# GpSimd adds the two states of six groups out of eight, not of four, ahead of TensorE's transposes into y

## The chip, the cores and the metric

The kernel runs on one core of a Trainium2 chip. The metric is the device time of one execution in microseconds. Before the change three runs gave 1902.42, 1903.18 and 1904.25 us, with a median of 1903.18 us. Engine names below are those of the profile: PE is TensorE's matmuls and PEld its weight loads, DVE is VectorE, ACT is ScalarE, POOL is GpSimd, SP is the engine whose queue issues the DMAs.

## The reference

A layer norm of x (4096 tokens, 256 channels, float32) goes into two branches, and their sum is added to x. One branch is a Mamba block (inner width 512, 16 states, a convolution of 4 taps), the other a local transformer of two layers (8 heads of 64, windows of 128 tokens, a gated MLP of hidden width 682). Cut to what the change touches, the Mamba branch:

```python
x_conv = silu(conv(x_inner) + conv_b)
x_dbl  = x_conv @ x_proj_w.T
dt     = softplus(x_dbl[..., :16] @ dt_proj_w.T + dt_proj_b)
B_ssm, C_ssm = x_dbl[..., 16:32], x_dbl[..., 32:48]
dA  = exp(dt[..., None] * A)                       # (l, 512, 16)
dBx = (dt * x_conv)[..., None] * B_ssm[:, None, :]
# for t in order:  h = dA[t] * h + dBx[t];  y[t] = sum over the 16 states of h * C_ssm[t]
y   = y + x_conv * D_param
out = y * silu(z) @ out_proj_w.T
...
return x + mamba(xn) + local_transformer(xn)
```

## The kernel before

The Mamba branch works on blocks of 512 tokens (`TB`, 8 of them) and on chunks of 128 inner channels (4 of them, on the partitions). For one block and chunk the 16 states are taken in 8 groups of two (`GS` = 8, `NG` = 2), so there are 8 x 4 x 8 = 256 groups in all. The transformer works on steps of 256 tokens, 16 for each of its two layers, 32 in all. Both branches run at once, interleaved on every engine.

One group is the function `recur` (line 775):

- L453 (called at 784): two DMAs on the SP queue copy two rows of B and two rows of C to all partitions, into two of the six buffers `bc` ("spreads"). A group holds two buffers, so three groups can be in flight. B's buffer is then written over and over: here it is called u.
- L793: POOL multiplies u (128 x 1024) by `dtx`, which is dt times x_conv.
- for each of the two states: L802 ACT makes the decay exp(dt A) into a PSUM tile `da` (there are two), L807 DVE scans along the tokens, L813 ACT keeps the last column for the next block, L817 DVE multiplies by C into the state's half of u.
- L825, only for groups whose number is in `PAIRED` (line 49): POOL adds the two halves of u into the first one.
- L829, `collect`: PE transposes 128 x 128 tiles of u and accumulates them in the PSUM tile y. There are four transposes for each half that is left: four for a paired group, eight for another. The lines are 823 to 840:

So over all groups and states y is summed by TensorE's accumulation of transposes; where a group is paired, one of its two additions is made by POOL. When the eight groups of a chunk are through, `close` (842) copies y (L846), turns it back (L850), adds x_conv D (L854) and gates it (L859), and `out_proj` (L879) follows after the four chunks. The other POOL work is in the steps of the softplus (L765, L767, L768), in the rotary products and sums of the transformer (L899, L945, L985), and in the MLP's norm and gate (L1149, L1157, L1218).

The order of instructions on each engine is fixed when the program is built, by the class `Plan`. Each piece of work is recorded with an engine, an assumed duration, what it reads and writes, and a key. The key is a place in the pipeline minus a lead, `soon=`, which stands at nearly every call. `Plan.order` (183) runs through the engines and picks, of the work that is ready by its own account of durations and buffers, the one with the smallest key, looking ahead by `AHEAD` at most. The result is five queues (PE, DVE, ACT, POOL, SP), each in order. On the chip an instruction at the head of a queue whose input or buffer isn't ready holds up all that is behind it.

```python
n_sums = 1 if g in PAIRED else NG
if n_sums == 1:
    add("POOL", 1.22, lambda: nc.gpsimd.tensor_tensor(u.ap[:, 0, :], u.ap[:, 0, :], u.ap[:, 1, :], ALU.add), [], [u], soon=-0.37)
...
for i in range(n_sums):
    add("PE", 0.44, lambda i=i: collect(i), [(u, i)], [y], soon=-0.06)
```

Of the kernel before, what the change touches and what calls it, by code (L numbers as in the profile page):

```python
# [42 lines left out]
AHEAD = 2.190000  # L43
# [5 lines left out]
PAIRED = (1, 3, 5, 7)  # L49
# [269 lines left out]
def mamba_and_local_transformer(  # L319
# [135 lines left out]
    def load_small():  # L455
        dma(96, lambda: xpw.ap, lambda: xp_wT.rearrange("(c p) n -> p c n", p=P), writes=[xpw], soon=-0.27)
        for at_row in (0, DH):
            dma(32, lambda at_row=at_row: dtw.ap[at_row : at_row + DTR], lambda: dt_wT, writes=[(dtw, at_row)], soon=-1.3)
        dma(128, lambda: b2row.ap, lambda: b2_d[DEPTH - 1 : DEPTH, :].partition_broadcast(P), writes=[b2row], soon=-0.91)

    def load_qkv(l):
        for s in range(3):
            cut = slice(s * INNER, (s + 1) * INNER)
            dma(
                512, lambda cut=cut: wqkv.ap[:, :, cut],
                lambda cut=cut: wqkv_d[l][:, cut].rearrange("(k p) n -> p k n", p=P), writes=[(wqkv, s)], soon=-0.18,
            )

    def load_rest(l):
        dma(512, lambda: wo.ap, lambda: wo_d[l].rearrange("(h p) n -> p h n", p=P), writes=[wo], soon=-0.99)  # L470
        for half in range(2):
            for m, n in ((0, WHOLE), (NM - 1, LAST)):
                to, of = w1_at(half, m), half * HID + m * MC
                dma(
                    n, lambda to=to, n=n: w1.ap[:, :, to : to + n],
                    lambda of=of, n=n: w1_d[l][:, of : of + n].rearrange("(k p) n -> p k n", p=P),
                    writes=[(w1, (half, m))], soon=0.35,
                )
# [3 lines left out]
            lambda: w2_d[l][0:whole, :].rearrange("(m p) n -> p m n", p=MC), writes=[(w2, 0)], soon=-0.25,  # L482
        )
        dma(42, lambda: w2.ap[0 : HID - whole, NM - 1, :], lambda: w2_d[l][whole:HID, :], writes=[(w2, 1)], soon=0.66)
# [28 lines left out]
        add("PE", 8.3, shift, [w1], [pb], soon=-0.7)  # L513
        add("DVE", 0.4, bias, [pb], [b1, b1x], soon=0.6)
        add("DVE", 4.6, scale, [], [w1], port=True, soon=0.34)
# [14 lines left out]
    def base_of(s):  # L530

        base = plan.value(rows_b)
        if s in sums:
            dma(256, lambda: base.ap, lambda: sums[s].ap, [sums[s]], [base], soon=-0.57)
            return base
        dma(256, lambda: base.ap, lambda: rows(x, s), writes=[base], soon=-1.31)
# [3 lines left out]
            ), [b2row], [base], soon=-0.48,  # L540
# [3 lines left out]
    def finish(s, po, base):  # L544

        add("DVE", 0.6, lambda: nc.vector.tensor_tensor(base.ap, halves(po), base.ap, ALU.add), [po], [base], soon=-1.48)  # L546
        if s in sums:
            dma(256, lambda: rows(out, s), lambda: base.ap, [base], soon=-0.51)
            return
        sums[s] = plan.fixed(dram.tile([P, NW, D], F32, tag=f"sum{s}", name=f"sum{s}"))  # L550
        dma(256, lambda: sums[s].ap, lambda: base.ap, [base], [sums[s]], soon=0.0)
# [4 lines left out]
    def shift_column(l, s):  # L556
        now = xts[l, s]
        if s == 0:
            add("POOL", 0.14, lambda: nc.gpsimd.memset(now.ap[:, 1, 0:1], 0.0), [], [(now, 0)], soon=0.0)
        else:  # L560
# [3 lines left out]
                [(old, 1)], [(now, 0)], soon=-0.52,  # L564
            )

    def normalize(s):
# [5 lines left out]
        dma(256, lambda: xb.ap, lambda: rows(x, s), writes=[xb], soon=0.37)  # L573
# [27 lines left out]
        add("DVE", 1.1, stats, [xb], [mv], soon=1.29)  # L601
        add("ACT", 0.5, root, [mv], [rstd], soon=0.53)
        add("DVE", 0.6, centre, [mv, rstd], [xb], port=True, soon=-0.03)
        now = xts[0, s] = plan.value(tokens)
        add("PE", 0.44, turn, [xb], [pt], holds=[now], soon=0.01)
        add("ACT", 0.48, lambda: nc.scalar.copy(now.ap[:, :, 1:], halves(pt)), [pt], [(now, 1)], soon=0.16)
        shift_column(0, s)
        dma(256, lambda: xn_d[s].ap, lambda: now.ap[:, :, 1:], [(now, 1)], [xn_d[s]], soon=-0.93)
# [3 lines left out]
    def reload(s):  # L612
        now = xts[1, s] = plan.value(tokens)
        dma(256, lambda: now.ap[:, :, 1:], lambda: x1_d[s].ap, [x1_d[s]], [(now, 1)], soon=-1.46)
# [6 lines left out]
    def in_half(i):  # L621
# [3 lines left out]
            lambda: in_wT[:, i * DI : (i + 1) * DI].rearrange("(k p) n -> p k n", p=P), writes=[w], soon=-1.21,  # L625
# [3 lines left out]
    def in_proj(b, w, c, to):  # L629
# [9 lines left out]
        add("PE", 1.72, emit, [w, xms[b]], [pm], holds=[to], soon=-0.6)  # L639
        return pm  # L640

    def front_load(b):
        xm = xms[b] = plan.value(xms_b)
        for i in range(PB):
            s = b * PB + i
            dma(
                256, lambda i=i: xm.ap[:, :, i * TS : (i + 1) * TS], lambda s=s: xn_d[s].ap, [xn_d[s]], [(xm, i)], soon=0.29
            )
# [4 lines left out]
    def front_conv(b, c, w):  # L653
        xin, xc, tail = plan.value(rows_m), xcs[b], tails[b]
        edge = slice(c * (TAPS - 1), (c + 1) * (TAPS - 1))
        if b == 0:
            add("POOL", 0.14, lambda: nc.gpsimd.memset(xin.ap[:, 0 : TAPS - 1], 0.0), [], [(xin, 0)], soon=0.12)
        else:
# [3 lines left out]
                [(old, c)], [(xin, 0)], soon=0.95,  # L662
            )
        pm = in_proj(b, w, c, xin)
        add("ACT", 0.48, lambda: nc.scalar.copy(xin.ap[:, TAPS - 1 :], pm.ap), [pm], [(xin, 1)], soon=0.73)
        if b < NB - 1:
            add(
                "POOL", 0.14, lambda: nc.gpsimd.tensor_copy(tail.ap[:, edge], xin.ap[:, TB:]), [(xin, 1)], [(tail, c)], soon=0.09
# [5 lines left out]
            ), [], [pm], soon=-0.15,  # L674
# [8 lines left out]
        for j in range(TAPS - 1):  # L683
            add("DVE", 0.7, lambda j=j: tap(j), [xin, pm], [(xc, c) if j == TAPS - 2 else pm], soon=0.78)

    def silu(v):
# [4 lines left out]
        add("ACT", 4.52, emit, [], [v], soon=0.43)  # L691

    def front_dbl(b):
# [3 lines left out]
        def emit():  # L697
# [9 lines left out]
        add("PE", 1.75, emit, [xc, xpw], [px], holds=[xd, part], soon=-0.32, part="columns")  # L707
        add("ACT", 0.48, lambda: nc.scalar.copy(part.ap[0:n, 0:TB], px.ap[DH : DH + n]), [px], [part], alone=[px], soon=0.25)
        add(
            "DVE", 0.6, lambda: nc.vector.tensor_tensor(xd.ap[0:n], px.ap[0:n], part.ap[0:n, 0:TB], ALU.add),  # L710
            [px, part], [(xd, 0)], alone=[px], soon=-1.5,
        )

        add("ACT", 0.48, lambda: nc.scalar.copy(xd.ap[DH : DH + DTR], xd.ap[0:DTR]), [(xd, 0)], [(xd, 1)], soon=-0.07)
        xds[b] = xd
        bc = bcs[b] = plan.fixed(dram.tile([2 * NS, TB], F32, tag=f"bc{b}", name=f"bc{b}"))
        dma(64, lambda: bc.ap, lambda: xd.ap[DTR:n, :], [(xd, 0)], [bc], soon=0.15)

    def gate_conv(b, c, w):
# [4 lines left out]
        add("ACT", 0.48, lambda: nc.scalar.copy(sz.ap[:, c, :], pz.ap), [pz], [(sz, c)], soon=-0.62)  # L724

    def times(b, c):
# [12 lines left out]
        add("PE", 1.15, emit, [xd, dtw], banks2, holds=dts2, soon=0.77, part="rows")  # L739
        for i in range(2):  # L740
# [3 lines left out]
                ), [banks2[i]], [dts2[i]], soon=0.17,  # L744
# [3 lines left out]
    def prepare(b, c):  # L748

        if c % 2 == 0:  # L750
# [7 lines left out]
        add("ACT", 0.6, lambda: nc.scalar.activation(e.ap[:, n], dt.ap, AF.Abs), [dt], [e], soon=-0.79)  # L758
        add("ACT", 0.6, lambda: nc.scalar.activation(dt.ap, dt.ap, AF.Relu), [], [dt], soon=-1.5)
# [3 lines left out]
            [e], [r], port=True, soon=0.0,  # L763
        )
        add("POOL", 1.22, lambda: nc.gpsimd.tensor_tensor(r.ap[:, n], e.ap[:, n], r.ap[:, n], ALU.subtract), [e], [r], soon=0.43)  # L765
        add("ACT", 0.6, lambda: nc.scalar.activation(e.ap[:, n], e.ap[:, n], AF.Ln, bias=one_t), [], [e], soon=0.53)
        add("POOL", 1.22, lambda: nc.gpsimd.tensor_tensor(dt.ap, dt.ap, r.ap[:, n], ALU.add), [r], [dt], soon=-1.5)  # L767
        add("POOL", 1.22, lambda: nc.gpsimd.tensor_tensor(dt.ap, dt.ap, e.ap[:, n], ALU.add), [e], [dt], soon=-0.88)  # L768
        add(
            "DVE", 0.61, lambda: nc.vector.tensor_tensor(dtx.ap, dt.ap, xc.ap[:, c, :], ALU.mult),  # L770
            [dt, (xc, c)], [dtx], port=True, soon=0.42,
# [3 lines left out]
    def recur(b, c, g):  # L775
# [6 lines left out]
        for s in range(2):  # L782
# [4 lines left out]
                .rearrange("n t -> (n t)").partition_broadcast(P), [bc], [w], soon=-0.78,  # L787
# [7 lines left out]
            ), [dtx], [u], soon=0.16,  # L795
        )
        for i in range(NG):
# [6 lines left out]
                ), [dt], [h], soon=0.96,  # L804
# [4 lines left out]
                ), [(u, i), (state, (c, n))], [h], soon=-1.03,  # L809
            )  # L810
            if b < NB - 1:
                add(
                    "ACT", 0.1, lambda h=h, n=n: nc.scalar.copy(state.ap[:, c, n : n + 1], h.ap[:, TB - 1 : TB]),  # L813
                    [h], [(state, (c, n))], alone=[h], soon=0.0,
# [4 lines left out]
                ), [h, spread[1]], [(u, i)], alone=[h], soon=-0.19,  # L819
# [4 lines left out]
        if n_sums == 1:  # L824
            add("POOL", 1.22, lambda: nc.gpsimd.tensor_tensor(u.ap[:, 0, :], u.ap[:, 0, :], u.ap[:, 1, :], ALU.add), [], [u], soon=-0.37)  # L825
# [13 lines left out]
        for i in range(n_sums):  # L839
            add("PE", 0.44, lambda i=i: collect(i), [(u, i)], [y], soon=-0.06)  # L840

    def close(b, c):
# [3 lines left out]
        add("ACT", 0.48, lambda: nc.scalar.copy(ytv(), y.ap), [y], [yt], soon=-0.97)  # L846

        def turn():
# [3 lines left out]
        add("PE", 0.44, turn, [yt], [py], soon=0.0)  # L852
# [3 lines left out]
            ), [py], [(xc, c)], soon=-1.5,  # L856
# [3 lines left out]
            [sz], [(xc, c)], soon=-1.24,  # L860
        )

    def out_load():
# [3 lines left out]
            writes=[w], soon=1.12,  # L867
# [3 lines left out]
    def out_proj(b, i, w):  # L871
# [12 lines left out]
        add("PE", 3.44, emit, [w, xc, base], [po], soon=-0.93)  # L884
# [5 lines left out]
    def rotation(l, s):  # L890
# [3 lines left out]
            writes=[rot], soon=0.02,  # L894
        )
        for i, scales in enumerate((qks, qkw)):
            for q in range(2):
# [6 lines left out]
                    ), [rot], [(trig, (i, q))], soon=-0.19,  # L904
# [3 lines left out]
    def project(l, s, t):  # L908
# [3 lines left out]
        def matmuls(q, holds):  # L912
# [10 lines left out]
            add("PE", 1.72, emit, [xb, (wqkv, q)], [pm], holds=holds, soon=0.19)  # L923
# [4 lines left out]
        def norm(q, pm, sq):  # L928
            add("ACT", 0.48, lambda: nc.scalar.activation(sq.ap, pm.ap, AF.Square), [pm], [sq], alone=[pm], soon=0.53)
# [3 lines left out]
                ), [sq], [(nrm, q)], soon=-0.7,  # L933
# [10 lines left out]
        def turned(parts, to):  # L944
            add("POOL", 1.22, lambda: nc.gpsimd.tensor_tensor(parts[0].ap, parts[0].ap, parts[1].ap, ALU.add), [parts[1]], [parts[0]], soon=1.16)  # L945
# [9 lines left out]
            add("PE", 0.44, emit, [parts[0]], [pt], holds=[to], soon=0.36)  # L955
# [458 lines left out]
```

## Time and profile before

| | |
|---|---|
| median of three runs | 1903.18 us |
| the profiled execution's own time | 1899.32 us |
| its span, first to last instruction | 1897.5 us |
| mean granted TensorE clock | 0.993 |
| busy: PE / PEld / DVE | 1855.4 / 1423.5 / 1724.6 us |
| busy: ACT / POOL | 1539.9 / 1410.9 us |
| L829 PE, transposes into y | 1536 instructions |
| L825 POOL, the addition of two states | 128 instructions |
| L793 POOL, u by dtx | 256 instructions, 606.0 us |
| L807 DVE, scans (two forms) | 512 instructions, 639.8 us |
| share of time in which the DMA queue's packets run | 52.5% |

The profile is that of one execution. A matmul's recorded duration overlaps the next one's, so the busy time of PE is larger than what PE must spend; the distance between the starts of matmuls that follow each other without a wait tells the latter. A row of groups has the line, engine, operation and shapes, the count, the busy time and the mean duration in ns of one, then the idle time ahead of these instructions and what ended it. A row of waits has who waited, for what, the total in us, the number of times and the longest.

### The profile page before, as it was taken

To read this page: it belongs to the slowest core of one execution; us is meant where nothing else is said; L and a number is where in the kernel's file an instruction comes from. 1 tells how busy PE (TensorE), PEld (TensorE's weight loads), DVE (VectorE), ACT (ScalarE), POOL (GpSimd) and SP (SyncE) were. 2 spreads that over 40 slices of the span, in tenths; PEclk is the share of its full clock that TensorE was granted. 3 is DMA by queue.
4 is the path that set the end of the run, shared out by engine and by line. 5 is a ranking of instruction groups with operands and counts; after the bars stand their busy time and mean duration, and the time that the engine had idled before them with its cause. 6 is when DMAs were issued, how large, how long until landed. Compare 5 with 4: busy or idle time off the path is not lost. (4 is left out here: it accounts for less than half of the span.)

```text
span 1897.5 us, 35612 instructions
## 1 busy us (share of the span) xinstructions
PE 1855.4 (98%) x12432; PEld 1423.5 (75%) x12432; DVE 1724.6 (91%) x3190; ACT 1539.9 (81%) x3634; POOL 1410.9 (74%) x1178
## 2 busy tenths in 40 slices
PE   7999999999999999999999999999999999999997
PEld 4777777877777778778778787778777787777786
DVE  6799999999998999989998898998999989998996
ACT  5897988888878788788886888888898878888773
POOL 3676888777877778867787676887768877787874
PEclk9999999999999999999999999999999999999998
DMA  5453655554555455555555644556444564544654
GB/s 188 139 194 114 221 166 180 180 173 166 198 167 182 145 170 194 163 187 185 191 184 191 216 152 162 169 189 222 152 160 163 191 214 159 180 160 155 217 173 144
DMA packets 133956, 334.69 MB, mean 176 GB/s; under 512 B 13468, under 2 KB 57200, under 8 KB 133776
## 3 DMA queue, kind: packets, MB, share of 16 engines
q1 hardware_dynamic: 133488, 332.21, 52.5%
q8 instruction: 98, 1.61, 0.3%
q14 instruction: 82, 0.67, 0.1%
q10 hardware_dynamic: 288, 0.20, 0.0%
HBM read 315.06 MB, written 17.30 MB: 175 GB/s over the span
## 5 line engine op out<-in xcount | busy, mean ns | idle before, releaser
L793 POOL TENSOR_TENSOR bc<-dtx,bc 128x1024 f32<-128x1024 f32 x256 | 606.0, 2369 | 144.1 <-DMA bc<-bc 107.1
L807 DVE TENSOR_TENSOR_SCAN da<-da,state,bc 128x512 f32<-128x512 f32 x448 | 563.5, 1278 | 39.7 <-ACT da L802 21.1
L802 ACT ACTIVATE da<-dt,negA 128x512 f32<-128x512 f32 x512 | 348.3, 693 | 78.4 <-DVE bc L817 74.9
L918 PE MATMUL mm<-wqkv,xt 128*128 128x512 f32 x768 | 355.1, 598 | 1.4 <-DVE top L1032 1.2
L817 DVE TENSOR_TENSOR bc<-da,bc 128x512 f32<-128x512 f32 x512 | 339.0, 678 | 5.7 <-ACT state L813 3.4
L1176 PE MATMUL mm<-hn,w 128*128 128x256 f32 (+1 forms) x1408 | 338.2, 383 | 1.3 <-DVE mlp L1226 0.5
L1176 PEld LDWEIGHTS mm<-hn,w 128*128 128x128 f32 (+1 forms) x1408 | 256.8, 189 | 60.2 <-issue 17.0
L1042 ACT ACTIVATE pr<-pr,top 128x256 f32<-128x256 f32 (+1 forms) x512 | 253.2, 500 | 25.9 <-DVE top L1032 25.6
L918 PEld LDWEIGHTS mm<-wqkv,xt 128*128 128x128 f32 x768 | 139.5, 191 | 133.4 <-issue 120.7
L825 POOL TENSOR_TENSOR bc<-bc 128x512 f32<-128x512 f32 x128 | 164.6, 1287 | 88.0 <-DVE bc L817 86.9
L829 PE MATMUL y<-ident,bc 128*128 128x128 f32 x1536 | 214.9, 277 | 8.8 <-POOL bc L825 8.3
L1032 DVE CUSTOM_DVE_ANT_0 pr<-mm,maskf,nrm 128x256 f32<-128x256 f32 (+1 forms) x512 | 213.1, 474 | 9.5 <-PE mm L1017 9.0
L985 POOL TENSOR_TENSOR turn<-turn,trig 128x512 f32<-128x512 f32 x128 | 162.9, 1293 | 65.7 <-DVE turn L978 57.1
L829 PEld LDWEIGHTS y<-ident,bc 128*128 128x128 f32 x1536 | 175.5, 142 | 46.6 <-issue 20.8
L945 POOL TENSOR_TENSOR turn<-turn,turn 128x512 f32<-128x512 f32 x128 | 164.6, 1286 | 51.3 <-DVE turn L963 50.8
L1017 PEld LDWEIGHTS mm<-kT,qT 64*128 64x128 f32 x2016 | 119.9, 187 | 36.1 <-issue 14.4
L1059 ACT COPY prT<-mm 128x512 f32<-128x512 f32 (+1 forms) x256 | 137.0, 591 | 7.0 <-PE mm L1055 6.3
L1055 PE MATMUL mm<-ident,pr 128*128 128x128 f32 x1008 | 135.7, 278 | 3.8 <-ACT qT L956 1.4
L813 ACT COPY state<-da 128x1 f32<-128x1 f32 x448 | 70.1, 165 | 85.1 <-DVE da L807 70.3
L1017 PE MATMUL mm<-kT,qT 64*128 64x128 f32 x2016 | 136.7, 281 | 0.0
L1071 PE MATMUL mm<-prT,v 128*64 128x128 f32 x2016 | 132.2, 278 | 0.7 <-ACT prT L1059 0.2
L1055 PEld LDWEIGHTS mm<-ident,pr 128*128 128x128 f32 x1008 | 117.6, 144 | 18.9 <-issue 4.9
(132 smaller groups left out, 3444.9 us busy)
## 6 DMA issues: line engine op xcount, KB each, us to landing
bc<-bc SPq DMA_DIRECT2D x512, 512.0 KB, 4.4
io<-in_x SPq DMA_DIRECT2D x32, 256.0 KB, 5.0
mw<-in_in_wT SPq DMA_DIRECT2D x16, 512.0 KB, 5.1
rot<-in_rot SPq DMA_DIRECT2D x32, 128.0 KB, 4.2
xn<-xt SPq DMA_DIRECT2D x16, 256.0 KB, 4.0
xm<-xn SPq DMA_DIRECT2D x16, 256.0 KB, 4.2
x<-mid SPq DMA_DIRECT2D x16, 256.0 KB, 3.0
mw<-in_out_wT SPq DMA_DIRECT2D x8, 512.0 KB, 3.7
```

The source lines that it names most:

```text
L793: "POOL", 2.35, lambda: nc.gpsimd.tensor_tensor(u.ap, dtx.ap.unsqueeze(1).to_broadcast([P, NG, TB]), u.ap, ALU.mult), [dtx], [u], soon=0.16,
L802: "ACT", 0.63, lambda h=h, n=n: nc.scalar.activation(h.ap, dt.ap, AF.Exp, scale=negA[:, c * NS + n : c * NS + n + 1]), [dt], [h], soon=0.96,
L807: "DVE", 1.18, lambda h=h, n=n, i=i: nc.vector.tensor_tensor_scan(h.ap, h.ap, u.ap[:, i, :], state.ap[:, c, n : n + 1] if b else 0.0, ALU. ...
L817: "DVE", 0.61, lambda h=h, i=i: nc.vector.tensor_tensor(u.ap[:, i, :], h.ap, spread[1].ap[:, i, :], ALU.mult), [h, spread[1]], [(u, i)], a ...
L825: add("POOL", 1.22, lambda: nc.gpsimd.tensor_tensor(u.ap[:, 0, :], u.ap[:, 0, :], u.ap[:, 1, :], ALU.add), [], [u], soon=-0.37)
L829: nc.tensor.matmul(y.ap[:, t, :], lhsT=u.ap[:, i, t * P : (t + 1) * P], rhs=ident, is_transpose=True, start=g == 0 and i == 0 and t == 0, ...
L918: nc.tensor.matmul(pm.ap, lhsT=hT[k], rhs=wqkv.ap[:, k, q * INNER : (q + 1) * INNER], start=k == 0, stop=k == KC - 1,)
L1017: nc.tensor.matmul(halves(scs[j])[:, i, a * WIN : (a + 1) * WIN], lhsT=qT.ap[half, 2 * g + i, :], rhs=kk.ap[half, 2 * g + i, :], start=n == 0,
L1032: nc.vector.tensor_tensor_reduce(out=prs[j].ap[:, i, keys], in0=halves(scs[j])[:, i, keys], in1=mask[:, keys], scale=nrm.ap[:, h : h + 1], ...
L1042: nc.scalar.activation(prs[j].ap[:, i, keys], prs[j].ap[:, i, keys], AF.Exp, bias=top.ap[:, h : h + 1], scale=-1.0, accum_out=den.ap[:, h ...
L1055: nc.tensor.transpose(ppv()[:, j, a, :], prs[j].ap[:, i, a * WIN : (a + 1) * WIN], ident)
L1176: nc.tensor.matmul(halves(pm)[0:r, i, :], lhsT=w1.ap[:, k, c0 : c0 + r], rhs=hn.ap[:, k, :], start=k == 0, stop=k == KC - 1,)
```

## The change

Line 49 takes groups 0 and 4 into `PAIRED`, so that six groups of eight are paired. In 64 groups more, two for each of the 32 pairs of block and chunk, POOL adds the halves, and PE has four transposes instead of eight. Besides, `AHEAD` and nearly all of the 119 leads have other values, so the order on all five queues is another one. The diff, cut to the lines the text speaks of:

```diff
-AHEAD = 2.190000
+AHEAD = 2.170000
...
-PAIRED = (1, 3, 5, 7)
+PAIRED = (0, 1, 3, 4, 5, 7)
...
-                    writes=[(w1, (half, m))], soon=0.35,
+                    writes=[(w1, (half, m))], soon=-1.38,
...
-                .rearrange("n t -> (n t)").partition_broadcast(P), [bc], [w], soon=-0.78,
+                .rearrange("n t -> (n t)").partition_broadcast(P), [bc], [w], soon=-0.81,
...
                 u.ap, dtx.ap.unsqueeze(1).to_broadcast([P, NG, TB]), u.ap, ALU.mult
-            ), [dtx], [u], soon=0.16,
+            ), [dtx], [u], soon=-0.07,
...
         if n_sums == 1:
-            add("POOL", 1.22, lambda: nc.gpsimd.tensor_tensor(u.ap[:, 0, :], u.ap[:, 0, :], u.ap[:, 1, :], ALU.add), [], [u], soon=-0.37)
+            add("POOL", 1.22, lambda: nc.gpsimd.tensor_tensor(u.ap[:, 0, :], u.ap[:, 0, :], u.ap[:, 1, :], ALU.add), [], [u], soon=-0.86)
...
         for i in range(n_sums):
-            add("PE", 0.44, lambda i=i: collect(i), [(u, i)], [y], soon=-0.06)
+            add("PE", 0.44, lambda i=i: collect(i), [(u, i)], [y], soon=-0.05)
...
-            add("POOL", 1.22, lambda: nc.gpsimd.tensor_tensor(parts[0].ap, parts[0].ap, parts[1].ap, ALU.add), [parts[1]], [parts[0]], soon=1.16)
+            add("POOL", 1.22, lambda: nc.gpsimd.tensor_tensor(parts[0].ap, parts[0].ap, parts[1].ap, ALU.add), [parts[1]], [parts[0]], soon=0.5)
```

In the orders that are built, POOL has on average 7.4 instructions between a group's multiplication (L793) and its addition (L825) before, and 9.0 after; 1.5 of them before and 1.8 after are multiplications of later groups. The first transpose into y stands behind 63.5 us of PE work before and behind 68.2 us after (each instruction counted with its distance between starts, see the prediction). On PE the 96 short matmuls of L495, which read w1, stand ahead of x_dbl's matmuls (L702) after, and behind them before; on the SP queue the four loads of w1 stand behind those of wo and w2 after, and ahead of them before. Behind the last transpose into y both orders have the same 7.8 us of PE work.

## The prediction

> **What bounds the kernel now.** I read the page first: busy times, then the costliest groups.
>
> ```profile
> span 1897.5 us, 35612 instructions
> PE 1855.4 (98%) x12432; PEld 1423.5 (75%) x12432; DVE 1724.6 (91%) x3190; ACT 1539.9 (81%) x3634; POOL 1410.9 (74%) x1178
> L793 POOL TENSOR_TENSOR bc<-dtx,bc 128x1024 f32<-128x1024 f32 x256 | 606.0, 2369 | 144.1 <-DMA bc<-bc 107.1
> L825 POOL TENSOR_TENSOR bc<-bc 128x512 f32<-128x512 f32 x128 | 164.6, 1287 | 88.0 <-DVE bc L817 86.9
> L829 PE MATMUL y<-ident,bc 128*128 128x128 f32 x1536 | 214.9, 277 | 8.8 <-POOL bc L825 8.3
> ```
>
> PE is busy nearly throughout, VectorE 91%; POOL has 487 us free. PE's busy time overstates its need, because a matmul's recorded duration overlaps the next. So I took the timeline of PE in a stretch without a wait and read the distances between starts.
>
> ```profile
> 911.92 0.60 PE L829 MATMUL y<-ident,bc 128*128 128x128 f32 x4
> 912.35 0.60 PE L950 MATMUL mm<-ident,turn 128*128 128x128 f32 x4
> 912.79 0.60 PE L1097 MATMUL mm<-ident,wide 128*128 128x128 f32 x4
> 913.32 2.02 PE L1071 MATMUL mm<-prT,v 128*64 128x128 f32 x32
> 915.27 0.66 PE L829 MATMUL y<-ident,bc 128*128 128x128 f32 x4
> 915.76 1.89 PE L1176 MATMUL mm<-hn,w 128*128 128x256 f32 x8
> 917.49 3.73 PE L1112 MATMUL mm<-OT,wo 128*128 128x128 f32 x32
> 921.06 0.60 PE L829 MATMUL y<-ident,bc 128*128 128x128 f32 x4
> ```
>
> Four transposes take 0.43 to 0.44 us (911.92 to 912.35), 0.109 us each, not the 0.277 of the row; eight matmuls of L1176 take 1.73 us, 0.216 each. Counting every PE group of the page with its distance (768 and 256 of 128x512 at 0.429, 2560 of 128x256 at 0.216, 3568 transposes at 0.109, 1024 of L1112 at 0.111, 2016 + 2016 small ones at 0.060 to 0.064, and some 40 us of the rest) gives 1786 us. PE thus has work for 94% of the span and stands idle 112 us: some 20 before the first transpose into y at 83.6, some 20 after 1850, the rest spread thinly, 7 to 19 us in each stretch of 237. PE is the bound, loosely.
>
> Third, the waits around the addition, SP's own among them:
>
> ```profile
> PEld y L829 <- POOL bc L825: 11.3, 8, 3.8
> PE y L829 <- POOL bc L825: 8.3, 3, 3.5
> POOL bc L825 <- DVE bc L817: 86.9, 42, 6.4
> POOL bc L793 <- DMA bc<-bc: 107.1, 74, 4.9
> DVE da L807 <- POOL bc L793: 12.0, 13, 2.6
> SPq L453 <- PE y L829: 496.7, 195, 8.9
> ```
>
> PE waited 19.6 us (11.3 and 8.3) for 128 additions. The last row says that loads into u are issued when the transposes have let the buffer go: a buffer freed later is a load issued later.
>
> **The change part by part.** *Transposes removed.* 64 groups (2 more of 8, 32 times) lose four each: 256 x 0.109 = 27.9 us off PE, all on the engine that is the bound. The 256 weight loads (142 ns each, 36 us of PEld) lie beside matmuls and count nothing; were they not covered, they would be inside the same 0.109.
>
> PE's row puts a transpose at 277 ns, and the Trainium skill, "TensorE: Matmul & The Clock Gate", Part 4: PE-mode transpose, has about 275 ns for one in a kernel's context; by that the 256 would be worth 70 us. The starts decide against it here: that duration is latency, and neighbours overlap it.
>
> *Additions added.* 64 x 1.287 = 82.4 us on POOL: 1410.9 to 1493, 79%. POOL's own free time hides it; without that cover it would be 82.4 us. What leaks is waiting:
> - PE for the additions. Two of the waits (3.8 and 3.5) are in the last 35 us, around groups that were paired before. Without them 12.3 us stand against some 126 additions, 0.097 each, so 64 more cost 6.2 us. Bounds: 0, and the whole 82.4 if each addition went through.
> - Work queued behind the new additions on POOL: the next groups' L793, the rotary sums L945, L985, and the softplus. For these VectorE waited 12.0 us (L807), PEld 11.6 (L950 for L945), ACT 6.5 (L766 for L765): 30 us. POOL's free time falls from 487 to about 387, a factor 1.26, and if the waits grow by it, 7.8 us come, of which I put half, 4, on PE's path. Bounds 0 to 7.8.
> - The addition waits for L817 at the head of POOL's queue (86.9 us in 128, 0.68 each): 43 us more of POOL standing, still within its free time. Nothing.
> - The buffer u is kept an addition longer; its next load, behind it in SP's queue, comes later. POOL already waits 107 us for such loads, yet only 12.0 us of that reach the scans. Taken as within the 4 us; the slow rival below prices it in full.
>
> VectorE and POOL get in each other's way in a few VectorE instructions:
>
> ```profile
> L770 DVE TENSOR_TENSOR dtx<-dt,xc x32: 673/785/1750, 69.5 to 1833.9; 128x512 f32<-128x512 f32 x32
> L762 DVE TENSOR_SCALAR m2k<-m2k x32: 370/432/2186, 64.6 to 1812.5; 128x512 f32<-128x512 f32 x32
> ```
>
> The three numbers are minimum, median and maximum. The means are 974 and 759 ns, so 32 each lose 9.6 and 12.4 us over the minimum; L589 (363 to a mean of 691, x32) and L972 (140 to 349, x64) lose 10.5 and 13.4. Together 46 us, while the scans and L817 (minimum 634, maximum 693) lose nothing. With POOL 5.8% busier that is 2.7 us more, on an engine with slack: 0 on the path, 2.7 at most.
>
> The Trainium skill, "SBUF — State Buffer", section "SBUF: two separate sides", speaks against giving POOL more: the port pair that it shares with VectorE is locked for a whole instruction and the loser fully blocks. If every VectorE instruction fell under it, 82 us of POOL would be up to 82 us of VectorE. The page limits it to perf modes or two SBUF inputs, and the rows agree: L770 reads two SBUF tiles, L817 has one operand in PSUM.
>
> *Leads and AHEAD.* No work is added, every order moves. At the start 68.2 us of PE work stand ahead of the first transpose into y instead of 63.5; if that fills idle time, 4.7 us are gained. Against it, PE now has L495 (5.2 us in the trace) ahead of L702, and its w1 is loaded after wo and the 640 KB of w2, which took 6.2 us to land; PE, in order, may stand there up to 5 us with L702, x_dbl and the first group behind it. Net 0, bounds -5 to +5. In the steady part the idle time of equal stretches differs between 7 and 19 us under one set of leads; I take 0, bounds -8 to +8. At the end both orders have the same 7.8 us behind the last transpose, and the last groups were paired already: 0.
>
> Sum: -27.9 + 6.2 + 4 = -17.7 us on a span of 1897.5, so 1879.8. The profiled execution took 1899.3, the median of the runs is 1903.18, 5.7 above the span; I carry that over: 1885.
>
> **The rivals.**
> 1. *All of it comes, and the new order closes gaps.* Waits don't grow, the start fills: -27.9 - 4.7, 1871. For it: POOL's 487 us free, PE's thin idle time that a new order can touch. Against it: PE did wait for additions already. 22 in 100.
> 2. *Another engine becomes the bound and nothing comes.* VectorE is busy 223 of 237 us in the stretch from 287 to 524; with 1.5% less PE work the same 223 stand in 233.5, 95.5%. If every microsecond that PE gains were spent waiting for VectorE, 1903, no change. Against it: VectorE's starts are closer than its durations too (L817: 0.598 to 0.678), so it has more slack than it shows. 7 in 100.
> 3. *The ring of buffers becomes the bound: slower.* Each of 64 groups frees u 1.287 us later or more, the load lands 4.4 us after its issue, L793 starts late, the scans and the transposes with it. A group saves 0.435 us of PE, so from a third of the addition (0.435 of 1.287) the change loses. At half, 64 x (0.644 - 0.435) = +13.3: 1916; at the whole, +54: 1958. For it: SP's 497 us of waiting for L829 and POOL's 107 for loads show that loads come just in time; the addition now stands behind more later multiplications. Against it: 12.0 us of waiting in the scans, and 0.097 for each paired group so far. 19 in 100.
>
> That the change doesn't do what it says is excluded by the orders: 192 additions and 1280 transposes.
>
> **How the numbers follow.** My forecast, 1885 (its own range 1874 to 1897, from the bounds of waits and leads), has 52 in 100. The range 1867 to 1908 takes in rivals 1 and 2, and the lower edge of 3; what it leaves out is most of 3 and a very good order. A change of 0.2%, 3.8 us, is about what can be told from none. Faster: 74 (52 + 22); slower: 18 of rival 3's 19; same: 8, rival 2 and the edge of 3.
>
> **What would show it.** After: L829 x1280, L825 x192 near 1287 ns, POOL near 1493 us, and PE's work, by starts, 1758 us. PE's idle time tells the rest: 112 before, about 122 by my forecast, below 112 by rival 1, 140 by rival 2 and over 150 by rival 3. PE's waits for L825 should go from 19.6 to about 26; POOL's waits for loads (107) and the scans' for L793 (12.0) stay near what they are, where rival 3 has them doubled. I am wrong if the scans' waits for L793 or for decays grow by tens of microseconds, or if L702 begins well after 48 us with PE standing ahead of L495.

## The result, and the profile after

The changed kernel is slower. Eleven runs of it have a median of 1909.34 us (1907.05 to 1915.46), eleven of the kernel before, run beside it, 1903.85 (1901.57 to 1907.28); the ratio is 1.0033, with a 95% interval of 1.0022 to 1.0043. The profiled execution of the changed kernel took 1915.46 us, the longest of the eleven, with a mean granted clock of 0.988.

The head of its page, and three of its costliest groups:

```profile
span 1913.5 us, 35254 instructions
PE 1850.4 (97%) x12176; PEld 1399.4 (73%) x12176; DVE 1735.0 (91%) x3190; ACT 1539.2 (80%) x3634; POOL 1485.6 (78%) x1242
L793 POOL TENSOR_TENSOR bc<-dtx,bc 128x1024 f32<-128x1024 f32 x256 | 605.8, 2368 | 163.2 <-DMA bc<-bc 113.0
L825 POOL TENSOR_TENSOR bc<-bc 128x512 f32<-128x512 f32 x192 | 245.7, 1283 | 65.4 <-DVE bc L817 59.9
L829 PE MATMUL y<-ident,bc 128*128 128x128 f32 x1280 | 187.6, 278 | 12.3 <-POOL bc L825 11.6
```

What was to be moved was moved: 256 transposes fewer, 64 additions more at 1283 ns, and POOL 75 us busier. PE's work, counted by starts as in the prediction, fell from 1785.7 to 1757.8 us, the 27.9 forecast. Yet the span is longer, so PE's idle time rose from 112 to 156 us (in executions near the medians it would be some 4 more before and some 6 less after). Counted so, idle time takes in what PE loses to a lower clock: a mean of 0.993 over 1897.5 us leaves out 13 us of full clock, a mean of 0.988 over 1913.5 us leaves out 23. So at most 10 of the 44 us more are slower matmuls, and the rest is waiting. The view of waits, where a row has the engine, what it waited for, the total in us, the count and the longest:

```profile
POOL bc L793 <- DMA bc<-bc: 113.0, 70, 5.1
POOL bc L825 <- DVE bc L817: 59.9, 38, 5.4
DVE da L807 <- ACT da L802: 37.2, 36, 3.5
PEld y L829 <- POOL bc L825: 16.5, 17, 5.7
ACT nrm L938 <- DVE nrm L972: 14.1, 12, 2.4
DVE da L807 <- POOL bc L793: 13.6, 14, 3.6
PE y L829 <- POOL bc L825: 11.6, 8, 5.4
```

PE's waits for additions are 28.1 us (16.5 and 11.6) against 19.6 before, near the 26 forecast. POOL's waits for loads and the scans' for L793 have hardly moved (107.1 and 12.0 before), so the ring of buffers isn't what got worse. One row stands out: the scans' wait for the decays (L807 for L802) was 21.4 us and is 37.2. ScalarE's wait for L972, a short VectorE instruction, was 5.2 us and is 14.1.

The second thing that changed is a set of VectorE instructions that last far longer than they need. The groups of the changed kernel by form:

```profile
L972 DVE TENSOR_SCALAR nrm<-nrm 128x16 f32<-128x16 f32 x64 | 33.8, 528 | 0.2
L589 DVE TENSOR_SCALAR io<-io,mv,rstd 128x256 f32<-128x256 f32 x32 | 30.3, 989 | 2.8 <-ACT rstd L585 2.8
L770 DVE TENSOR_TENSOR dtx<-dt,xc 128x512 f32<-128x512 f32 x32 | 29.5, 923 | 7.6 <-POOL bc L793 7.6
L762 DVE TENSOR_SCALAR m2k<-m2k 128x512 f32<-128x512 f32 x32 | 18.7, 584 | 2.2 <-ACT m2k L760 2.2
```

The minima of the four are 141, 355, 670 and 409 ns. With mean minus minimum, times the count, L972 loses 24.8 us, L589 20.3, L770 8.1 and L762 5.6: 59 us, against 46 before. L972, the floor under the norms of q and k, works on 16 numbers a partition and lasts up to 2354 ns. The timeline around one such case (start, duration, engine, line):

```profile
162.00 2.36 POOL L793 TENSOR_TENSOR bc<-dtx,bc 128x1024 f32<-128x1024 f32 x1 [0.52 <-DMA bc<-bc]
162.28 2.11 DVE L972 TENSOR_SCALAR nrm<-nrm 128x16 f32<-128x16 f32 x1
...
164.42 0.21 ACT L938 ACTIVATE nrm<-nrm 128x16 f32<-128x16 f32 x1 [1.96 <-DVE nrm L972]
164.67 0.31 ACT L939 ACTIVATE nrm<-nrm,lift_t 128x16 f32<-128x16 f32 x1
164.88 0.67 ACT L802 ACTIVATE da<-dt,negA 128x512 f32<-128x512 f32 x1
...
165.49 1.06 ACT L1059 COPY prT<-mm 128x512 f32<-128x512 f32 x2
...
166.12 0.70 PE L635 MATMUL mm<-xm,mw 128*128 128x512 f32 x1 [1.97 <-ACT prT L1059]
```

L972 starts while POOL's L793 runs and ends at 164.39, 0.03 us after it. An instruction that lasts on so until POOL's is through is called held here. Of the 64 L972, 24 last over 1.5 times the minimum, and each of them ends 0.03 us after an instruction on POOL; the held ones of L589, L762 and L770 each end 0.15, 0.28 and 0.55 us after one. ScalarE, in order, waits 1.96 us for it with the decay and two copies queued behind, and PE stands 1.97 us for one of those copies. PE's granted clock, in the windows that follow (start and end, length, PE busy with its count, clock, DMA share, GB/s):

```profile
160.00:165.00 5.00, 4.15 (x32) 1.00 0.28 97
165.00:170.00 5.00, 3.88 (x12) 0.68 0.62 210
170.00:175.00 5.00, 5.00 (x28) 0.98 0.41 107
```

So a hold of an instruction that needs 0.14 us can reach PE through ScalarE, and the pause is followed by matmuls at a lower clock. Whether this is what the change cost, the experiments must show.

### The profile page after: what moved, and what is told of

Read it like the earlier page. It is cut to its first block, busy times and chain, and to the rows that moved or that the text cites. A ratio compares the mean times of both kernels' runs of the same rounds, so it can differ in the third digit from the quotient of the medians.

```text
span 1913.5 us, 35254 instructions
## 1 busy us (share of the span) xinstructions
PE 1850.4 (97%) x12176; PEld 1399.4 (73%) x12176; DVE 1735.0 (91%) x3190; ACT 1539.2 (80%) x3634; POOL 1485.6 (78%) x1242
## 5 line engine op out<-in xcount | busy, mean ns | idle before, releaser
L793 POOL TENSOR_TENSOR bc<-dtx,bc 128x1024 f32<-128x1024 f32 x256 | 605.8, 2368 | 163.2 <-DMA bc<-bc 113.0
L807 DVE TENSOR_TENSOR_SCAN da<-da,state,bc 128x512 f32<-128x512 f32 x448 | 562.4, 1277 | 50.1 <-ACT da L802 30.2
L802 ACT ACTIVATE da<-dt,negA 128x512 f32<-128x512 f32 x512 | 348.5, 692 | 67.8 <-DVE bc L817 65.1
L918 PE MATMUL mm<-wqkv,xt 128*128 128x512 f32 x768 | 360.6, 600 | 1.8 <-ACT prT L1059 0.7
L825 POOL TENSOR_TENSOR bc<-bc 128x512 f32<-128x512 f32 x192 | 245.7, 1283 | 65.4 <-DVE bc L817 59.9
L945 POOL TENSOR_TENSOR turn<-turn,turn 128x512 f32<-128x512 f32 x128 | 164.5, 1285 | 61.2 <-DVE turn L963 60.9
L829 PE MATMUL y<-ident,bc 128*128 128x128 f32 x1280 | 187.6, 278 | 12.3 <-POOL bc L825 11.6
L829 PEld LDWEIGHTS y<-ident,bc 128*128 128x128 f32 x1280 | 147.3, 142 | 49.7 <-issue 19.3
L813 ACT COPY state<-da 128x1 f32<-128x1 f32 x448 | 71.6, 165 | 93.7 <-DVE da L807 86.5
L1059 ACT COPY prT<-mm 128x512 f32<-128x512 f32 (+1 forms) x256 | 136.7, 585 | 12.0 <-PE mm L1055 10.8
L1071 PE MATMUL mm<-prT,v 128*64 128x128 f32 x2016 | 137.8, 281 | 4.9 <-ACT state L813 4.5
L1071 PEld LDWEIGHTS mm<-prT,v 128*64 128x64 f32 x2016 | 113.4, 137 | 37.0 <-issue 10.6
```

The source lines that it names most:

```text
L793: "POOL", 2.35, lambda: nc.gpsimd.tensor_tensor(u.ap, dtx.ap.unsqueeze(1).to_broadcast([P, NG, TB]), u.ap, ALU.mult), [dtx], [u], soon=-0.07,
L802: "ACT", 0.63, lambda h=h, n=n: nc.scalar.activation(h.ap, dt.ap, AF.Exp, scale=negA[:, c * NS + n : c * NS + n + 1]), [dt], [h], soon=1.04,
L807: "DVE", 1.18, lambda h=h, n=n, i=i: nc.vector.tensor_tensor_scan(h.ap, h.ap, u.ap[:, i, :], state.ap[:, c, n : n + 1] if b else 0.0, ALU. ...
L829: nc.tensor.matmul(y.ap[:, t, :], lhsT=u.ap[:, i, t * P : (t + 1) * P], rhs=ident, is_transpose=True, start=g == 0 and i == 0 and t == 0, ...
L918: nc.tensor.matmul(pm.ap, lhsT=hT[k], rhs=wqkv.ap[:, k, q * INNER : (q + 1) * INNER], start=k == 0, stop=k == KC - 1,)
L1071: nc.tensor.matmul(hpair(po.ap)[j * DH : (j + 1) * DH, hp, :], lhsT=vv.ap[:, h * DH : (h + 1) * DH], rhs=prT.ap[:, j, a, :], start=a == first,
```

## The experiments

The times of several sittings are compared as ratios to the kernel before, run beside each; "us" below, where it is a difference, is a difference of ratios times 1902, the kernel before's usual median beside these runs. The intervals of the ratios are 1.6 to 4.3 us on either side. The changed kernel wasn't run again beside the later runs: its ratio is always the 1.0033 of the result.

Theory A was that the pairing costs the time, through POOL's additions, and theory B, its rival, that the new order does, whatever the work. Theory P came after the first runs: VectorE's instructions that POOL holds make the difference. The last runs have a theory D, and a P of another meaning, said where they stand.

**The two parts of the change apart.** First the pairing with the old leads, and the new leads with the old pairing, each ordered anew by `Plan.order`.

```diff
-PAIRED = (1, 3, 5, 7)          # the kernel before, its leads kept: old6
+PAIRED = (0, 1, 3, 4, 5, 7)
-PAIRED = (0, 1, 3, 4, 5, 7)    # the changed kernel, its leads kept: new4
+PAIRED = (1, 3, 5, 7)
```

> The kernel before with one line changed: PAIRED = (0, 1, 3, 4, 5, 7); all leads and AHEAD as before. Theory A (the additions themselves cost what they save: buffers freed later, queues on POOL): about as slow as the changed kernel, 1904 to 1915 us, whatever the leads. Theory B (the pairing brings what the forecast said, and the new order of all queues gives it back): 1880 to 1892 us.

> The changed kernel with one line changed back: PAIRED = (1, 3, 5, 7); new leads and AHEAD. Theory A: as the kernel before, 1900 to 1907 us, since the leads don't matter. Theory B: slower than the changed kernel by what the transposes cost, 1920 to 1935 us.

old6 took 1979.89 us, 1.0403 [1.0380, 1.0425]; new4 1942.10, 1.0204 [1.0187, 1.0222]. Both theories missed both numbers. Either set of leads is good for its own pairing only: when `PAIRED` changes, the whole order on all five queues changes. So these runs don't measure a part of the change. The next three hold the order fixed: every piece of work is still recorded and placed, and only what it issues is altered.

**The work apart, at the new order.** In the first, the 64 new additions issue nothing (the second state of groups 0 and 4 is missing in y); in the second the additions stay and the 256 transposes are put back (that state counts twice); the third has both edits, which is the instructions of the kernel before in the order of the changed one.

```diff
-lambda: nc.gpsimd.tensor_tensor(...)
+lambda: None if g in (0, 4) else nc.gpsimd.tensor_tensor(...)
...
-lambda i=i: collect(i)
+lambda i=i: ([collect(1)] if g in (0, 4) else []) + [collect(i)]
```

> The changed kernel, every queue in the same order, but the 64 additions of groups 0 and 4 are left out (the second state of these groups is then missing from y). Theory A: the wait for them goes and the saving shows, 1875 to 1890 us. Theory B: little changes, 1900 to 1908 us.

> The changed kernel, every queue in the same order, with the 64 additions kept and the 256 transposes that they replaced put back next to the others (the second state of groups 0 and 4 is counted twice in y). If PE's work decides, as the forecast assumed: 27.9 us more, 1937 us. If a loop through POOL, DVE and the buffers decides (theory A): far less, 1909 to 1920 us.

> Exactly the instructions of the kernel before (128 additions, 1536 transposes) in the queues' order of the changed kernel: the 64 additions of groups 0 and 4 are left out and their second halves transposed next to the first. If the order alone is the loss (theory B): 1922 to 1930 us, the run with both (1930) less the 5 us that leaving out the additions gave. If the order is as good as the old one and the pairing is what costs: 1900 to 1906 us.

Without the additions 1904.48 us, 1.0015 [1.0000, 1.0031]; with additions and transposes 1930.02, 1.0131 [1.0109, 1.0153]; old work in the new order 1923.36, 1.0116 [1.0097, 1.0136]. The first is what theory B expected, the third what the order alone as the loss would give, and the second lies between its two expectations. So the 64 additions cost some 3.4 us (1.0033 less 1.0015, which the intervals don't tell from nothing), the 256 transposes are worth 18.6 (1.0131 less 1.0033), and the pairing as a whole gains 15.8 (1.0116 less 1.0033). What is slower is the order: the same instructions take 22.1 us more in it.

**The holds.** Is it the held instructions that make the order dear? L972 was replaced by an instruction of the same numbers of another kind, in both kernels: a reduction over an axis of length one.

```diff
-nc.vector.tensor_scalar_max(nrm.ap, nrm.ap, NORM_MIN**2)
+nc.vector.tensor_reduce(nrm.ap, nrm.ap.unsqueeze(2), AX.X, ALU.max)
```

(The floor itself is left out.)

> The changed kernel, same orders, with L972 (the floor under the squared norms, 128 x 16 on VectorE) replaced by a VectorE reduction over an axis of length one, which leaves the values as they are (none is near the floor) and, if it is like the reciprocal L1088, is never held while POOL runs. Theory P (VectorE is held by POOL's instructions, and the new order has more of it: 24.8 us in L972 against 13.4 before): 1885 to 1900 us, a gain of more than the kernel before makes. Rival (holds are hidden, the loss comes from the longer queue on POOL and ACT): 1905 to 1910 us, as the changed kernel.

> The kernel before, same orders, with the same replacement in L972. Theory P: 1890 to 1898 us, 5 to 13 us less, some half of what the changed kernel gains. Rival: 1901 to 1905 us.

The changed kernel then takes 1902.14 us, 0.9997 [0.9985, 1.0009], a gain of 6.8; the kernel before 1899.34, 0.9992 [0.9981, 1.0003], a gain of 1.5 that is within its interval. Both times lie between the ranges of theory P and of its rival: this line's holds count in the new order, for less than P had it. The pause shown above is gone: L972 now takes 0.16 us at 161.97, L938 follows at 162.16, PE's L635 starts without a wait at 163.87, and ScalarE's waits for L972 are 3.6 us in all, not 14.1. L972's line, in the changed kernel and with the reduction (minimum, median, maximum in ns):

```profile
L972 DVE TENSOR_SCALAR nrm<-nrm x64: 141/165/2354, 17.8 to 1813.1; 128x16 f32<-128x16 f32 x64
```

```profile
L972 DVE TENSOR_REDUCE nrm<-nrm x64: 135/160/171, 17.9 to 1802.9; 128x16 f32<-128x16 f32 x64
```

In the same places of the same order the reduction is never held. This agrees with the Trainium skill, "SBUF — State Buffer", section "Who interferes with whom": the lock is taken by VectorE's `tensor_scalar` in a faster mode and by instructions with two SBUF inputs, and never by `tensor_reduce`.

Shorter POOL instructions should hold VectorE less long, so L793 was issued as two of 128x512:

```diff
-nc.gpsimd.tensor_tensor(u.ap, dtx.ap.unsqueeze(1).to_broadcast([P, NG, TB]), u.ap, ALU.mult)
+[nc.gpsimd.tensor_tensor(u.ap[:, i, :], dtx.ap, u.ap[:, i, :], ALU.mult) for i in range(NG)]
```

> The changed kernel, same orders, with each of POOL's 256 multiplications L793 (2.37 us, 128 x 1024) issued as two of 128 x 512, so that POOL holds VectorE for at most half as long at a time. Theory P: holds of about 2 us fall to about 1, 63 us in all to 40 or less, and the time to 1890 to 1902 us. Rival: 256 more instructions on POOL, 1907 to 1920 us.

1908.10 us, 1.0033 [1.0021, 1.0046]: nothing, as the rival had it. The held time of the four lines fell only from 59 to 52 us. Here L972 lasts up to 3704 ns, longer than any single POOL instruction: that one starts at 1376.81 while an L793 runs, and ends 0.03 us after the third POOL instruction in a row (L793, L793, L825). With the next one queued at once, the held one didn't get in between.

Then all four kinds were replaced by such reductions, in both kernels (the centring L589, the softplus' rounding term L762 and dt times x_conv L770 are left out; the reductions are not shorter than what they replace, but L589's no longer waits for rstd, 2.8 us in the changed kernel and 0.7 before, so that "without holds" takes this in too).

> The changed kernel, same orders, with all four kinds of VectorE instruction that POOL holds (L589, L762, L770, L972) replaced by reductions over an axis of length one on the same tiles; the layer norm's centring, the rounding term of the softplus and the product dt x_conv are left out by that. Theory P: holds of 63 us go to next to nothing and the time to 1883 to 1896 us, at least 13 us less than the changed kernel. Rival (holds matter little beyond L972's): 1899 to 1904 us.

> The kernel before, same orders, with the same four replaced. Theory P: 3 to 8 us less than the kernel before, 1894 to 1899 us, so that the changed kernel without holds is no slower than this one. Rival: holds cost both alike, the difference of 5 to 7 us stays.

The groups of the changed kernel so:

```profile
L762 DVE TENSOR_REDUCE m2k<-m2k 128x512 f32<-128x512 f32 x32 | 21.8, 680 | 2.1 <-ACT m2k L760 2.1
L770 DVE TENSOR_REDUCE dtx<-dt 128x512 f32<-128x512 f32 x32 | 21.8, 680 | 7.6 <-POOL bc L793 7.6
L589 DVE TENSOR_REDUCE io<-io 128x256 f32<-128x256 f32 x32 | 11.7, 407 | 0.0
L972 DVE TENSOR_REDUCE nrm<-nrm 128x16 f32<-128x16 f32 x64 | 10.6, 166 | 0.2
```

The changed kernel falls to 1889.00 us, 0.9932 [0.9919, 0.9946], a gain of 19.2; the kernel before to 1895.74, 0.9968 [0.9956, 0.9981], a gain of 6.1. Without holds the change is a gain of 6.8 us; with them it is a loss of 6.3. And the order without holds, with the kernel before's work:

> The instructions of the kernel before in the changed kernel's order (as in neworder_oldwork), with the four held kinds of VectorE instruction replaced as in after_allfree (the same parts of the computation left out). It says how much of the order's loss (1923.4 against 1902) is left without holds. If holds are all of it: 1894 to 1898 us, as before_allfree, and the pairing is then worth only 6 to 7 us. If the order is also worse by itself: 1901 to 1908 us, 6 to 12 above before_allfree, and the pairing is worth 12 to 19 in this order, as it was with holds (14).

1908.81 us, 1.0040 [1.0026, 1.0054], just above the higher of the two ranges. That completes a table, all times as ratio times 1902:

| | old order, old work | new order, old work | new order, new work |
|---|---|---|---|
| with holds | 1902.0 | 1924.1 | 1908.3 |
| the four kinds replaced | 1895.9 | 1909.6 | 1889.1 |
| what the holds cost | 6.1 | 14.5 | 19.2 |
| held beyond the minimum, four lines | 46 | 43 | 59 |

The order costs 13.7 us without holds and 22.1 with them; the pairing gains 20.5 without and 15.8 with them (this last difference is within the intervals). The last row says something that I hadn't thought of. Its 43 is from these rows of the new order with old work, with minima of 359, 143, 673 and 406 ns:

```profile
L589 DVE TENSOR_SCALAR io<-io,mv,rstd 128x256 f32<-128x256 f32 x32 | 27.6, 905 | 2.8 <-ACT rstd L585 2.7
L972 DVE TENSOR_SCALAR nrm<-nrm 128x16 f32<-128x16 f32 x64 | 26.7, 417 | 0.2
L770 DVE TENSOR_TENSOR dtx<-dt,xc 128x512 f32<-128x512 f32 x32 | 25.8, 806 | 5.6 <-POOL bc L793 5.6
L762 DVE TENSOR_SCALAR m2k<-m2k 128x512 f32<-128x512 f32 x32 | 16.6, 517 | 2.1 <-ACT m2k L760 2.1
```

The kernel before has as much time in holds, 46 us, as its work has in the new order, and pays less than half for it: 6.1 us, give or take 2.4, against 14.5, give or take 4.6. What a hold costs depends on where it falls, not on the sum alone.

**Versions meant to be kept.** Two tries at taking holds away in a way that could be kept. In the kernel before, the floor is folded into the bias of the logarithm L938, where it is added, and L972 isn't issued; in the changed kernel with L972 as a reduction (which still leaves the floor out, though its expectation speaks of the whole computation) the centring L589 goes to ScalarE, as three instructions for each half.

```diff
-add("DVE", 0.08, lambda: nc.vector.tensor_scalar_max(nrm.ap, nrm.ap, NORM_MIN**2), ...)
+add("DVE", 0.08, lambda: None, ...)
...
-nrm.ap, nrm.ap, AF.Ln, scale=65536.0
+nrm.ap, nrm.ap, AF.Ln, bias=floor_t, scale=65536.0
```

> The kernel before, same orders, with the floor under the squared norms put into the bias of the logarithm (L938) instead of a VectorE instruction (L972): the whole computation, 64 VectorE instructions and their holds fewer. Theory P: 1895 to 1900 us. Rival: 1901 to 1904 us.

> The changed kernel with the whole computation: L972 as in after_unlocked, and the layer norm's centring (L589, 20 us of holds) made by ScalarE, in three instructions for each of 32 halves, at the same place. Theory P: 1892 to 1900 us, below both kernels. Rival (ScalarE's extra work, some 25 us, comes to the place of the holds): 1902 to 1908 us.

1901.10 us, 0.9994 [0.9986, 1.0003], no change that can be told; and 1913.53, 1.0067 [1.0052, 1.0082], worse than without it (1902.14), and worse than either theory had it. ScalarE's busy time rose from 1539 to 1567 us, and work of its queue lies on the way to PE; that this is the reason wasn't tested apart. No version tried with all of the computation beats the kernel before by more than can be measured.

**What the order costs without holds.** The row of waits that had stood out, VectorE for the decays, goes with the order: here it is with old work and no holds, in the new order and then in the old.

```profile
DVE da L807 <- ACT da L802: 40.2, 40, 3.8
```

```profile
DVE da L807 <- ACT da L802: 23.4, 23, 7.0
```

So that coupling was taken away in both (theory D: these waits are what makes the new order worse by itself): L802 writes to a tile that nobody reads, and the scan takes what stands in its own PSUM tile (decays are left out of the scans).

```diff
-h.ap, dt.ap, AF.Exp, scale=...
+junk, dt.ap, AF.Exp, scale=..., saturate=False
...
-h.ap, h.ap, u.ap[:, i, :], ..., ALU.mult, ALU.add
+h.ap, h.ap, u.ap[:, i, :], ..., ALU.max, ALU.min
```

> The order of before, its work, the four held kinds replaced as in the run without holds (1895.7), and besides the coupling of the scans to the decays taken away: L802 writes its decays into a tile that nobody reads, and the scan L807 takes what stands in its own PSUM tile, with max and min in place of times and plus so that the numbers stay finite. Left out of the computation: centring, softplus rounding term, dt times x_conv, and the decays in the scans. VectorE's 23.4 us of waits for L802 must be gone. Theory D (the waits for decays are what makes the new order worse by itself): this one gains little, 1888 to 1896, since its order has few of these waits. Rival: the same here; the two differ in the next kernel.

> The same edit in the changed kernel's order with before's work and without holds (1908.8, 13.1 us above before's order). VectorE's 40.2 us of waits for L802 must be gone. Theory D: the two orders come within 4 us of each other, so this one at 1888 to 1899. Rival (the 13 us lie in many small waits of PE and in the granted clock after PE's pauses, and VectorE's waits for decays are hidden): the difference stays, 9 to 16 us, so this one at 1899 to 1910.

The old order took 1895.45 us, 0.9975 [0.9966, 0.9985], the new 1909.31, 1.0045 [1.0031, 1.0058]. The waits are gone and the difference is 13.3 us, as before. So theory D fails: the row that stood out is not the cause.

Next, PE's longest pause that only the new order has. The timeline of PE in the new order without holds, with old work:

```profile
223.42 0.67 PE L1071 MATMUL mm<-prT,v 128*64 128x128 f32 x8
228.64 1.13 PE L1071 MATMUL mm<-prT,v 128*64 128x128 f32 x8 [4.55 <-ACT state L813]
229.70 1.12 PE L1097 MATMUL mm<-ident,wide 128*128 128x128 f32 x4
230.60 1.06 PE L950 MATMUL mm<-ident,turn 128*128 128x128 f32 x4
```

PE waits for a copy on ScalarE (L1059; the view names L813, the copy right behind it) that stands behind a Gelu (L1213) and two loads of activation tables of 1.28 us, 4.05 us in all. Theory P of these runs is that this pause, with the lower clock behind it, is a large part of the order's price. This Gelu, the third of 32, was left out in both orders; and in a third kernel, the changed one with L972 as a reduction, it was moved behind the four instructions that followed it.

```diff
-for w in self.order():
-    w.emit()
+order = self.order()
+skip = [w for w in order if w.emit.__name__ == "gelu"][2]
+for w in order:
+    if w is not skip:
+        w.emit()
```

> The changed kernel's order with before's work and without holds (1908.8), and the third of the 32 Gelus (L1213 and the table loads around it, 4.05 us of ScalarE from 223.3 to 227.4) left out: that step's hidden values go on without it. In this order PE stands 4.5 us at 228 because L1059, queued behind that Gelu, comes late, and its granted clock is 0.76 to 0.90 from 220 to 240. Theory P (this one pause, with the clock behind it, is a large part of the order's 13 us): 1899 to 1904. Rival (later slack takes it up, the 13 us are spread): 1906 to 1910.

> The same Gelu left out in before's order without holds (1895.7), as the control: there it runs from 218.2 to 222.3 and PE has no pause behind it. Both theories: 1893 to 1897, a gain of 2 us at most; if it gains as much as the other kernel, the pause isn't what the Gelu's going is worth.

> The changed kernel with the floor on VectorE as a tensor_reduce (1902.1), and on ScalarE's queue the third Gelu put behind the four instructions that followed it (L802, L1059, L813, L1090), so that PE's L1071 and L1097 needn't wait for it; the whole computation. Theory P: a part of the 4.5 us pause and of the slower clock goes, 1896 to 1900. Rival: POOL's L945, which ends at 229.4, holds PE at L950 instead, and the Gelu's readers come later: 1901 to 1905.

1908.54 us, 1.0033 [1.0022, 1.0045]; 1895.74, 0.9968 [0.9957, 0.9978]; 1904.17, 1.0004 [0.9991, 1.0018]. Leaving the Gelu out saves the new order 1.3 us, within the intervals, and moving it saves nothing. The same place without the Gelu (the edit shifts line numbers by 3: L1074, L1100 and L953 are L1071, L1097 and L950) shows why:

```profile
224.48 0.66 PE L1074 MATMUL mm<-prT,v 128*64 128x128 f32 x8
227.06 0.67 PE L1074 MATMUL mm<-prT,v 128*64 128x128 f32 x8 [1.91 <-ACT state L816]
227.66 0.66 PE L1100 MATMUL mm<-ident,wide 128*128 128x128 f32 x4
230.57 1.11 PE L953 MATMUL mm<-ident,turn 128*128 128x128 f32 x4 [2.26 <-POOL turn L948]
```

A pause of 1.91 us is left, and a second of 2.26 has come: PE now waits for POOL's rotary sum (L945 of the kernels before). That sum ends at 230.51, against 229.45 with the Gelu, but the whole stretch begins 1.06 us later in this execution (L702 at 222.04, against 220.98), so counted from there the sum ends where it did, and PE passes the place some 1.1 us sooner. The long pause had two holders, and with one away the other takes over. So the run didn't take the pause away, and what it is worth isn't shown; nor where the rest of the order's 13 us lies. By starts, PE's idle time without holds is larger in the new order in four of six equal stretches of 237 us between 287 and 1709 (11.6, 6.8, 12.9, 11.0, 7.2 and 6.2 us, against 7.1, 11.1, 8.4, 9.5, 6.0 and 6.3), 7 us in sum. At most some 4 us are the clock: a mean of 0.991 over 1906.8 us leaves out 17 us of full clock, 0.993 over 1895.2 us leaves out 13. That the rest is spread is as far as these runs go.

## Why the prediction was wrong

The forecast was a change of -17.7 us, the result is one of +6.3, so 24.0 us are to be accounted for. By the table, the pairing without holds gave 2.8 more than forecast (20.5), the order by itself took 13.7, and the holds took 13.1 more than before (19.2 against 6.1): 13.7 + 13.1 - 2.8 = 24.0.

- *Transposes removed, 27.9 us.* PE's work fell by just that, and the time by 18.6 at the fixed order. The row's 277 ns a piece would have been 71 us; the starts were the right measure, but a microsecond off PE was worth only about two thirds of one in the time, so the term was 9.3 us too large.
- *Additions and what is queued behind them, 6.2 + 4.* PE's waits for L825 came out at 28.1 against 26 forecast, and the additions cost 3.4 us of the time, which isn't clear of noise. Right in kind, and about three times too dear.
- *The sum of the two, -17.7.* The pairing measured -15.8 with holds, -20.5 without. This sum was right, with some luck: 9.3 us too much for the transposes and 6.8 too much for the additions nearly cancel.
- *Leads and AHEAD: "I take 0, bounds -8 to +8", with -5 to +5 at the start.* This step failed first. The order cost 13.7 us by itself, 22.1 with holds, beyond the sum of both upper bounds. The bounds came from the spread of PE's idle time between stretches of one order, and that spread says how uneven one tuned order is, not how much worse another is. The sum had no term, either, for the clock that PE is granted, which went from 0.993 to 0.988 in the profiled executions.
- *VectorE and POOL: "0 on the path, 2.7 at most".* This step failed second. I scaled 46 us of holds by POOL's 5.8% and took VectorE's slack as cover. The holds rose to 59 us, and their price in the time from 6.1 to 19.2. Of these 13.1 us the order alone brought 8.4 (14.5 less 6.1); the other 4.7, with the work that was added, are within the intervals. The cover isn't VectorE's free time but the slack of whoever reads the held result: in the case shown, ScalarE's queue and through it PE. I did name the lock as speaking against the change, and then priced it by shares.
- *The rivals.* Rival 3, the slower one, was wrong in its mechanism: POOL waited for loads, and the scans for L793, hardly longer than before (113.0 and 13.6 us, against 107.1 and 12.0). PE's idle time of 156 us was in the range I gave to it, "over 150", so that sign couldn't tell a late buffer from a late anything. The scans' waits for decays, named as a sign of being wrong, grew by 16 us, and weren't the cause. The start, for which I feared L702 behind L495, plays no part: L702 begins at 43.0 us, against 48.1 before, and the first transpose into y at 87.0, against 83.6, with 4.7 us more work ahead of it.

## What to carry to other kernels

A change of work that brings a new order has two prices, and the second can be measured by itself: issue the old work in the new order. An order that was tuned for one set of work isn't an order for another (with six groups paired, the kernel is 77 us slower than before with the old leads and 6 with the new), so "no work is added" is no reason for a zero. And a short instruction that another engine can hold is priced by who waits for its result, in each place where it falls; a sum of held time, or a share, doesn't tell.

## What the runs showed of the hardware

- A VectorE instruction of 0.14 us lasted up to 3.70 us while POOL ran one instruction after another. In the changed kernel all 24 of its long instances ended 0.03 us after an instruction on POOL. Cutting POOL's instruction in two took the held time of four lines only from 59 to 52 us and changed nothing in the time, and a reduction over an axis of one was never held (178 ns at most in this place).
- PE's granted clock can fall to half after a pause of 2 us. After the pause of 1.97 us that ended at 166.12 it was 0.50 in each microsecond from 167 to 170, and 1.00 again from 171; after one of some 4.5 us that ended at 232.5, 0.50 from 232 to 238. Summed over the windows from 166 to 171 and from 231 to 239, the clock lost is 1.7 and 3.4 us, which is the most that it cost beyond the pause. It doesn't always fall: in the new order with old work the same pause, 1.95 us up to 166.27, was followed by the full clock (1.00 from 166 to 170), and so was one of 1.87 us up to 1665.77 in the changed kernel (1.00 from 1666 to 1670). What decides it, these runs don't tell. The Trainium skill, "TensorE: Matmul & The Clock Gate", Part 1, gives an idle window of about 3.4 us as what brings the half clock; here it came after 2 us.
